# Finished rows handled by pairs, stores on ScalarE's queue, w1's left operands partly in place and left2 held in program order, in a fused graph-attention kernel

## The chip, the cores and the metric

The kernel runs on one core of a Trainium2 chip. The metric is the device time of one execution in microseconds (us); the number quoted for a kernel is the median of its runs. The kernel before takes 1988.92 us, the median of four runs from 1987.42 to 1991.52 on the chip that also ran the changed kernel. (The prediction used 1990.13, the median of three earlier runs.)

## The reference, cut to what matters

Two graph layers on x (4096 x 512), each with a residual and a row norm. The second layer sets the closing stage:

```python
# layer 1; x is the output of layer 0, adj is 4096 x 4096
node_att = softmax(x @ node_w, axis=0)
e = (x @ edge_w) @ (x @ edge_w).T
edge_att = softmax(where(adj > 0, e, NEG_BIG), axis=1)
output = (adj * (node_att * edge_att)) @ (x @ weight) + bias
x = layernorm(x + output)
```

## The kernel before: the parts concerned

The large products are done by Strassen's scheme (seven half-size products in place of eight), which needs sums and differences of operand quarters. Nothing here turns on the algebra; what matters is that TensorE waits for operands which VectorE combines, and that DMAs bring and fetch.

From about 1088 us on the kernel forms the weighted sums `bank <- rop, lop` in sixteen blocks (g, r): four groups g of four blocks. When a group is complete, its rows are *finished*: multiplied with w1 (`po`), added to the residual rows (`xb`), normed and stored. This finishing is cut into small steps (a queue `todo`) that are taken between the sums of the next group, one step for each 8 units of work.

All left operands lie in a pool of four buffers, `lopp`. Three kinds of tile share it before the change: the loads of `lop`, `left2` (combinations of a lop, made by VectorE in the first group only, then stored to memory for the later groups), and `left1` (combinations for w1).

```python
def lefts(self, m, lop):                       # only for g == 0
    s = lopp.tile([P, 4, BG // 2, P], F32, name="left2", tag="lop")
    nc.vector.tensor_add(s1, l21, l22)         # L954
    nc.vector.tensor_sub(s2, s1, l11)          # L955
    nc.vector.tensor_sub(s3, l11, l21)         # L956
    nc.vector.tensor_sub(s4, l12, s2)          # L957
    yield
    nc.scalar.dma_start(to[:, :2]..., lop[:, :, :P])   # ScalarE's queue
    nc.scalar.dma_start(to[:, 2:6], s)
    nc.scalar.dma_start(to[:, 6], l22)
# ...
class Finish:                                  # four row blocks of 128 rows
    def steps(self):
        yield self.load                        # four xb loads, SyncE's queue
        for q in range(2):
            yield from self.pair(q, ps_tr)     # rows (q, q + 2): combine, 7 products
        yield lambda: self.norm(range(BG))     # root, scale and store of all four
# ...
    nc.sync.dma_start(out[...], xb)            # in norm, SyncE's queue
```

The order on each engine is not the order of the program: a scheduler places instructions, except those that are wrapped in `tc.keep_in_program_order`. Before the change that is, in the closing stage, the preparation of operands in the first block (`pinned[0]` is that wrapper for block 0 and does nothing afterwards).

## Time and profile before

Lines L1061 and L1183 of the kernel before are L1062 and L1189 of the changed one (sums and w1 products); L954 to L957 are L955 to L958 (left2); L823 and L835 (mask addition and weighting of the next block's operands) keep their numbers.

My measure throughout is *loss*: the sum of all start-to-start distances of TensorE's records in excess of its own median for the same size (0.429 us for 512 columns, 0.216 for 256, 0.109 for 128). It counts idle time and half-clock time alike. It leaves out places whose excess adds up to 0.1 us or less.

| kernel before, profiled run | loss of TensorE, us |
|---|---|
| 600 to 1083 us (scores, with the hole near 1010) | 12.4 |
| 1083 to 1300 us (first group of blocks) | 7.8 |
| after 1300 us (three holes of 10.6, 11.8 and 12.2 among them) | 44.1 |

The timeline of the kernel before, VectorE and then TensorE (start, length, engine, line, operation, out<-in, shapes, count, and in brackets the idle time before it with what ended it; DVE is VectorE, PE TensorE, ACT ScalarE, POOL GpSimd, SP SyncE, and a q marks the issue of a DMA):

```profile
1167.36 0.43 DVE L954 TENSOR_TENSOR left<-lop 128x256 f32<-128x256 f32 x1 [0.60 <-PE bank L1061]
...
1170.57 0.42 DVE L957 TENSOR_TENSOR left<-lop,left 128x256 f32<-128x256 f32 x1
...
1173.11 2.28 DVE L823 CUSTOM_DVE_ANT_1 lent<-lent,line 128x2048 f32<-128x2048 f32 x1
...
1190.00 8.80 PE L1061 MATMUL bank<-slot,lop 128*128 128x512 f32 x16 [2.07 <-DMA lop<-lop_d]
```

VectorE makes left2 *ahead of* the mask addition L823. ScalarE stores it at 1171.02, that store lands at 1183.93, only then are buffers of the pool free, and SyncE issues three lop loads (1183.99). TensorE waits 2.07 us for the first. So even before the change this chain, left2, store, free buffer, lop load, had no slack at all.

### The profile page before, as it was taken

How to read it: one execution, taken by the hardware profiler on the slowest of the kernel's cores; microseconds unless marked ns; L12 is line 12 of the kernel's file. 1: busy time of each engine (PE TensorE's matmuls, PEld its weight loads, DVE VectorE, ACT ScalarE, POOL GpSimd, SP SyncE). 2: the span in 40 equal slices, each digit the busy share in tenths (PEclk: the TensorE clock that was granted, in tenths of full speed). 3: DMA queues.
4: the chain of work that ended last, by engine and by line, in shares of the span. 5: the costliest groups of instructions: out<-in, count | busy, mean ns of one | idle time of the engine just before them, and what ended most of it. 6: DMA issues, size and time to landing. Idle time of an engine off the chain costs nothing.

```text
span 1990.7 us, 20142 instructions
## 1 busy us (share of the span) xinstructions
PE 1934.7 (97%) x6742; PEld 1210.0 (61%) x6742; DVE 1386.4 (70%) x2050; ACT 1006.0 (51%) x1596; POOL 299.3 (15%) x424
## 2 busy tenths in 40 slices
PE   9999999999999999999989999999899989999898
PEld 6888888888544455545445444466565656666555
DVE  7767667667664575667456974977569866998537
ACT  5433333333104576666567564656656564755621
POOL 0122222223231111111021111110101110111000
PEclk9999999999999999999999999999899999999899
DMA  8888888887465585778598998776668775877621
GB/s 308 301 319 308 305 323 304 306 328 258 171 237 206 201 295 222 262 257 284 204 378 281 338 326 293 261 263 235 240 241 308 259 262 179 318 261 249 247 78 64
DMA packets 153223, 521.82 MB, mean 262 GB/s; under 512 B 15008, under 2 KB 24224, under 8 KB 145440
## 3 DMA queue, kind: packets, MB, share of 16 engines
q1 hardware_dynamic: 66528, 232.68, 34.3%
q0 software_dynamic: 66912, 247.49, 33.4%
q10 hardware_dynamic: 19680, 40.38, 5.7%
q8 instruction: 53, 0.87, 0.2%
q14 instruction: 50, 0.41, 0.1%
HBM read 389.94 MB, written 130.55 MB: 261 GB/s over the span
## 4 chain that ended last, share of the span: by engine, by line
PE 73%; issue 9%; DMA 9%; DVE 6%; ACT 3%; POOL 1%; POOLq 0%; SPq 0%; DVEq 0%; ACTq 0%
PE bank L1061 23%; PE seven L702 13%; PE acc L374 11%; PE acc L373 11%; PE pe L633 4%; PE seven L101 3%; PE po L1183 2%; PE pt L603 2%; DMA slot<-in_adj_t_dram 1%; DMA lop<-lop_d 1%; DMA slot<-s_d 1%; DMA lent<-in_adj_t_dram 1%; DMA out_dram<-xb 1%; PE acc L246 1%; PE pt L333 1%
## 5 line engine op out<-in xcount | busy, mean ns | idle before, releaser
L1061 PE MATMUL bank<-lent,lop 128*128 128x512 f32 (+1 forms) x1292 | 430.6, 485 | 10.8 <-DMA lop<-lop_d 7.7
L373 PE MATMUL acc<-xw,hi 128*128 128x512 f32 x960 | 376.4, 392 | 0.0
L374 PE MATMUL acc<-xw,lo 128*128 128x512 f32 x960 | 374.2, 390 | 0.0
L1061 PE MATMUL bank<-slot,lop 128*128 128x512 f32 (+1 forms) x896 | 349.8, 538 | 3.9 <-DMA lop<-lop_d 2.1
L1061 PEld LDWEIGHTS bank<-lent,lop 128*128 128x128 f32 x1292 | 247.9, 192 | 168.9 <-issue 137.8
L1061 PEld LDWEIGHTS bank<-slot,lop 128*128 128x128 f32 x896 | 171.2, 191 | 157.5 <-issue 142.6
L363 ACT CAST hi<-at 128x1024 fp32r<-128x1024 f32 x120 | 126.4, 1054 | 203.3 <-PE acc L373 148.4
L365 DVE TENSOR_TENSOR lo<-at,hi 128x1024 fp32r<-128x1024 f32 x120 | 146.9, 1224 | 85.2 <-ACT hi L363 85.2
L374 PEld LDWEIGHTS acc<-xw,lo 128*128 128x128 f32 x960 | 180.3, 188 | 37.1 <-DVE lo L365 0.3
L373 PEld LDWEIGHTS acc<-xw,hi 128*128 128x128 f32 x960 | 180.2, 188 | 36.7
L1070 ACT COPY over<-bank 128x512 f32<-128x512 f32 x200 | 114.2, 580 | 143.5 <-PE bank L1061 139.3
L633 PE MATMUL pe<-hT 128*128 128x512 f32 (+3 forms) x384 | 134.3, 493 | 0.0
L574 ACT ACTIVATE line<-line,nmax_c 128x512 f32<-128x512 f32 x160 | 114.9, 725 | 21.8 <-DVE nmax_c L565 21.7
L829 ACT ACTIVATE slot<-slot 128x2048 f32<-128x2048 f32 x40 | 76.5, 1912 | 97.0 <-DMA slot<-in_adj_t_dram 84.9
L565 DVE CUSTOM_DVE_ANT_0 line<-lent,slot 128x512 f32<-128x512 bf16 x144 | 93.1, 688 | 46.6 <-ACT slot L643 22.4
L823 DVE CUSTOM_DVE_ANT_1 slot<-slot,line 128x2048 f32<-128x2048 f32 x36 | 82.2, 2284 | 20.1 <-DMA slot<-s_d 18.7
L1194 DVE SCALAR_TENSOR_TENSOR xb<-po,f,xb 128x256 f32<-128x256 f32 x84 | 40.1, 478 | 75.1 <-PE po L1183 44.9
L826 ACT ACTIVATE slot<-slot 128x2048 f32<-128x2048 f32 x36 | 68.7, 1911 | 45.5 <-DVE slot L823 45.3
L633 PEld LDWEIGHTS pe<-hT 128*128 128x128 f32 x384 | 65.7, 194 | 42.0 <-issue 35.0
L702 PE MATMUL seven<-hT 128*128 128x512 f32 x192 | 89.8, 593 | 0.0
L603 PEld LDWEIGHTS pt<-ident,lent 128*128 128x128 f32 x412 | 51.8, 143 | 61.0 <-issue 46.8
L1037 ACT COPY bank<-over 128x512 f32<-128x512 f32 x144 | 84.4, 593 | 7.1 <-DMA lop<-lop_d 3.1
(258 smaller groups left out, 2879.4 us busy)
## 6 DMA issues: line engine op xcount, KB each, us to landing
at<-in_adj_t_dram SPq DMA_DIRECT2D x60, 1024.0 KB, 6.6
lop<-lop_d SPq DMA_DIRECT2D x112, 512.0 KB, 4.6
slot<-in_adj_t_dram POOLq DMA_DIRECT2D x42, 1024.0 KB, 7.0
slot<-s_d POOLq DMA_DIRECT2D x36, 1024.0 KB, 7.7
s_d<-slot POOLq DMA_DIRECT2D x33, 1024.0 KB, 6.9
lent<-s_d POOLq DMA_DIRECT2D x28, 1024.0 KB, 7.3
lent<-in_adj_dram SPq DMA_DIRECT2D x48, 512.0 KB, 5.1
s_d<-lent POOLq DMA_DIRECT2D x48, 512.0 KB, 4.5
```

What stands on the lines that cost most here:

```text
L363: nc.scalar.copy(hi, aq)
L365: nc.vector.tensor_sub(lo, aq, hi.bitcast(F32))
L373: nc.tensor.matmul(acc, hi[:, c, :], xw[:, kb, :], start=(kb == 0), stop=False)
L374: nc.tensor.matmul(acc, lo[:, c, :], xw[:, kb, :], start=False, stop=(kb == NB - 1))
L565: nc.vector.tensor_tensor_reduce(line, mask, src, -1.0, HUGE, ALU.add, ALU.min, accum_out=nmax_c[:, b, c : c + 1])
L574: nc.scalar.activation(line, line, AF.Exp, bias=nmax_c[:, b, c : c + 1], scale=-1.0, accum_out=sum_c[:, b, c : c + 1])
L603: nc.tensor.transpose(pt[:, j, :], src[:, ts(j, P)], ident)
L633: nc.tensor.matmul(pe[:, lo * P :], hT[:, k, ts(A * BG + i, P)], hT[:, k, (B * BG + lo) * P : (B + 1) * W], start=(k == 0), stop=(k == KD ...
L702: nc.tensor.matmul(ps, left[m][:, k, q, :], right[m][:, k, :], start=(first and k == 0), stop=(k == KD // 2 - 1), skip_group_check=not first,)
L1037: nc.scalar.copy(self.bank[:, : self.w], self.to())
L1061: nc.tensor.matmul(ps, lop[:, k, :], rop[:, k, :], start=start, stop=(k == K - 1), skip_group_check=True)
L1070: nc.scalar.copy(self.to(), self.bank[:, : self.w])
```

## The change

The intent: no block of four stores and four loads in front of the lop loads in SyncE's queue; rows of the other half loaded earlier; fewer tiles in the pool; and left2 held in program order, so that in the first block it no longer runs ahead and blocks VectorE's queue near 1010 us. The diff, cut to its core:

```diff
 def lefts(self, m, lop):
-    nc.vector.tensor_add(s1, l21, l22)
-    ...
+    tc.keep_in_program_order(nc.vector.tensor_add(s1, l21, l22))
+    tc.keep_in_program_order(nc.vector.tensor_sub(s2, s1, l11))
+    tc.keep_in_program_order(nc.vector.tensor_sub(s3, l11, l21))
+    tc.keep_in_program_order(nc.vector.tensor_sub(s4, l12, s2))
 ...
-def steps(self):
-    yield self.load
+def steps(self, then):
     for q in range(2):
         yield from self.pair(q, ps_tr)
-    yield lambda: self.norm(range(BG))
+        some = q, q + 2
+        yield lambda some=some: self.norm(some)
+        yield lambda some=some: (self.scale(some), then and then.load(some))
 ...
 def combine():
-    s.append(lopp.tile([P, 4, KD // 2, P], F32, name="left1", tag="lop"))
-    (four combinations into it)
+    lines.append(take(free_e)); left = lines[0].rearrange(...)   # not from lopp
+    s.extend((l21, s2, s3, l12))
+    nc.vector.tensor_sub(s3, l11, l21)
+    nc.vector.tensor_add(l21, l21, l22)
+    nc.vector.tensor_sub(s2, l21, l11)       # the fourth comes four products later
 ...
-    nc.sync.dma_start(out[...], xb)
+    nc.scalar.dma_start(to, xb)
 ...
-    while owed[0] >= 8: owed[0] -= 8 ...
+    while owed[0] >= 6: owed[0] -= 6 ...
```

There are more steps than before (a norm and a scale for each pair), which is why they come every 6 units of work; with 8 some would be left over at the end and the kernel doesn't build. The joins of inner sums also move one step later (`inner_next`).

## The prediction

> **What bounds the kernel now.** I read the page first, then TensorE's timeline over the closing stage (from 1088 us: the weighted sums in blocks, with the closing rows' products with w1 threaded between them), then the queues' timelines around each hole that it shows. The page says that TensorE is the bound almost everywhere:
>
> ```profile
> PE 1934.7 (97%) x6742; PEld 1210.0 (61%) x6742; DVE 1386.4 (70%) x2050; ACT 1006.0 (51%) x1596; POOL 299.3 (15%) x424
> ```
>
> So the change can only win the holes in TensorE's row, and what follows them. TensorE's timeline shows its pace where nothing waits: a record of 256 columns every 0.216 us (four in 0.86 us), one of 512 every 0.429 us. Comparing every start-to-start distance with this pace, I find 64 us lost after 600 us, 44 us of it after 1290 us, and three holes hold most of that. The first, on TensorE and on SyncE's queue (start, length, engine, line, out<-in, count, idle before):
>
> ```profile
> 1404.73 1.03 PE L1061 MATMUL bank<-slot,lop 128*128 128x256 f32 x4
> 1413.43 3.75 PE L1061 MATMUL bank<-lent,lop 128*128 128x256 f32 x8 [7.67 <-DMA lop<-lop_d]
> 1416.98 1.91 PE L1061 MATMUL bank<-slot,lop 128*128 128x256 f32 x4
> 1418.68 1.18 PE L1183 MATMUL po<-line,left 128*128 128x256 f32 x4
> ...
> 1395.85 2.45 SPq L1238 DMA_DIRECT2D out_dram<-xb  x4
> 1398.35 9.20 SPq L1152 DMA_DIRECT2D xb<-x_d  x4
> 1407.61 0.42 SPq L1049 DMA_DIRECT2D lop<-lop_d  x1
> ```
>
> TensorE waits for left operands (lop). Their load stood in SyncE's queue behind four stores of finished rows (which waited for ScalarE's norm) and four loads of the other half's rows into the same four buffers (which waited for those stores to land). From 1404.73 to the next row at 1419.69 are 14.96 us for 20 records, worth 4.3 us: 10.6 us lost, although the idle is 7.67. The rest is the clock (columns: window, length, busy of PE, PEld, DVE, ACT, POOL, granted clock, DMA share, GB/s):
>
> ```profile
> 1405.00:1414.00 9.00, 1.33 (x6) 0.84 (x5) 4.50 (x5) 5.54 (x9) 0.00 (x0) 0.71 1.04 401
> 1414.00:1419.00 5.00, 5.00 (x13) 4.01 (x12) 2.67 (x3) 1.25 (x3) 0.00 (x0) 0.50 0.17 66
> 1639.00:1648.00 9.00, 7.88 (x13) 3.95 (x14) 8.37 (x7) 1.91 (x1) 0.00 (x0) 0.52 0.45 178
> 1862.00:1870.00 8.00, 6.88 (x12) 3.33 (x11) 8.00 (x13) 1.91 (x1) 0.00 (x0) 0.53 0.36 140
> ```
>
> After each hole TensorE runs some 5 to 8 us at half clock. The other two holes are the same traffic, seen from its other end: here the products wait for VectorE's addition to xb, and that for the late load.
>
> ```profile
> 1626.34 3.19 SPq L1238 DMA_DIRECT2D out_dram<-xb  x4
> 1633.02 2.26 SPq L1152 DMA_DIRECT2D xb<-x_d  x4
> ...
> 1638.30 0.48 DVE L1194 SCALAR_TENSOR_TENSOR xb<-po,f,xb 128x256 f32<-128x256 f32 x1 [8.75 <-DMA xb<-x_d]
> ...
> 1638.84 2.08 PE L1183 MATMUL po<-line,left 128*128 128x256 f32 x4 [6.43 <-DVE xb L1194]
> ...
> 1854.54 2.30 SPq L1152 DMA_DIRECT2D xb<-x_d  x4
> ...
> 1861.35 2.07 PE L1183 MATMUL po<-line,left 128*128 128x256 f32 x4 [7.14 <-DVE xb L1194]
> ```
>
> By the same subtraction the second loses 11.8 us (20.83 us from 1631.39 to 1652.22, with 10 records of 256 and 16 of 512 worth 9.0), the third 12.2 us. A fourth hole lies earlier, where the left combinations of the first block were moved forward by the scheduler and block VectorE's queue:
>
> ```profile
> 1014.74 0.43 DVE L954 TENSOR_TENSOR left<-lop 128x256 f32<-128x256 f32 x1 [9.84 <-DMA lop<-lop_d]
> ...
> 1017.03 1.08 PE L603 MATMUL pt<-ident,lent 128*128 128x128 f32 x4 [6.08 <-DVE lent L747]
> ```
>
> It costs 9.2 us: 6.2 idle and 3.0 slow.
>
> **What the Trainium skill says.** "TensorE: Matmul & The Clock Gate", Part 1: The HAM clock gate, has the clock halve after an idle window of about 3.4 us and come back after about as long a busy one. The trace agrees: 0.50 to 0.53 after idles of 7 us; so a removed hole of 7 us is worth 10 to 12. "DMA: Bandwidth & Descriptors", Anatomy of one DMA, has any semaphore wait sit on the issuing sequencer before dispatch: so one waiting issue holds all behind it, which is what SyncE's queue shows. The same page, Issuing engines are not separate DMA queues, says that issuing from another engine saves only the sequencer's time: the stores gain nothing in transport (2.7 us median here), only in not standing before the lop loads. "ScalarE: Activation LUTs", What ACT_TABLE_LOAD costs: 1283 ns; the trace has 1283 ns for each.
>
> **The change part by part.** *Pairs, and stores on ScalarE's queue.* The same 24 stores and 24 loads of 256 KB. Now rows (0, 2) are normed when their pair is done, stored from ScalarE's queue, and the other half's rows (0, 2) are loaded into their buffers while pair (1, 3) is still multiplied (eight steps). So the load has a whole pair of time, and no store stands in SyncE's queue. The loads still do, each waiting for a store to land, so I looked at the built order of the changed kernel and counted TensorE's work at the pace above. The first pair's last product ends 241 us after the first sum; the load that needs its buffers stands behind a lop load whose buffer TensorE frees only at 252, and the lop behind it is first used at 274. Norm, scale and store cost about 10 us from the page's and timeline's durations (table 1.28, root 0.3, two scalings of 0.8, landing 2.7, queueing), so the loads hardly wait, and 20 us remain for what is behind. For the second pair: 270, 283, 309. The third and fourth: 302, 309, 330 and 334, 344, 365. Later groups look alike. All three holes should go: 10.6 + 11.8 + 12.2 = 34.6 us.
>
> *Left combinations of w1 in place.* As many VectorE operations (four of about 0.42 us per pair), but no buffer of the pool of four that the lop loads use: lops can be a full four ahead. No hole names this, so I count 0; it makes the first item safer.
>
> *left2 held in program order.* VectorE's block at 1004 to 1014 goes. But in the built order ScalarE still has, before its copy of the transposes, two stores of that same lop, which wait for its landing at about 1014.7. TensorE then goes on a few us further until transpose buffers run out. I count 2.5 of the 9.2 us.
>
> *Six more norm groups.* ScalarE gets 6 more roots with two table loads each, 6 x (2 x 1.28 + 0.3) = 17 us, and 24 DMA issues of about 0.4 us (as its other issues show), 10 us. It is busy 385 of the 700 us after 1290: 412 is no bound.
>
> *Steps every 6 units of work instead of 8, inner joins one step later.* Every fourth step comes right behind another. Neighbouring steps use different banks, but VectorE has less time to add before a bank is used again: its queue has 2.28 us operations, and small waits for xb (1.73, 0.72) are there already. The later joins spare VectorE waits for ScalarE's copies (15.1 us off the path). I count 3 us of new small waits.
>
> Sum: 34.6 + 2.5 - 3 = 34 us, from 1990 to 1956. About 1.7%.
>
> **The rivals.** *The load now blocks the queue.* If norm and store come 10 us later than I think, xb loads hold the lops again: each of some 12 pair loads could cost up to 5 us, and the result would be 1970 or worse. For it: the loads stand in the same queue still. Against it: the distances above. *The next wait takes the place.* While TensorE stood, VectorE, ScalarE and the big operand loads caught up; without holes the next block's operands may be late. For it: small waits for operand combinations exist (0.33 at 1549, where no large hole is near). Against it: VectorE has 517 busy of these 700 us, 78% if the stretch shrinks by 35. It would return 5 to 15 us: 1961 to 1971. *TensorE waits for VectorE in the denser steps.* Up to 8 us more: 1964. *All goes.* If the fourth hole and the small ones also vanish, 34.6 + 9.2 + some 5: 1942. For it: small waits after 1290 add to 7 us, some from VectorE's backlog.
>
> **Range and chances.** A 2% gain needs 1950.3, 6 us below my point, and asks for most of the fourth hole or no new waits. The large term is well measured; only the new waits are guessed, so the range leans little: 1946 to 1968. Faster by over 2%: 0.22; within 2%: 0.77; slower: 0.01.
>
> **What would show it.** Right: no wait of TensorE over 3 us after 1290, the three half-clock stretches gone, VectorE's waits for the xb load near 0 (30.1 us now), stores on ScalarE's queue beside it. Partly right: TensorE still idles 2 to 4 us near 1010, with ScalarE's store as the cause. Wrong: TensorE waiting for lop loads behind xb loads; or waits for operands or bank copies spread over the blocks, adding to more than 10 us.

## The result, and the profile after

The changed kernel takes 1966.15 us (median of four runs, 1959.41 to 1972.42). Ratios in this document are the mean time of one kernel's runs over that of the other's of the same rounds, so not quite the ratio of the quoted medians: here 0.9884, 95% interval 0.9847 to 0.992. The class, within 2%, and the range hold; the point, 1956, was 10 us too low. The four runs spread over 13 us; the kernel before spreads over 4 us in its four, but over 12 us in the eleven runs timed beside e1 to e4, so the spread by itself says little.

The line of engines on the page of the changed kernel:

```profile
PE 1926.4 (98%) x6742; PEld 1206.2 (61%) x6742; DVE 1389.8 (71%) x2062; ACT 1021.8 (52%) x1614; POOL 300.1 (15%) x424
```

TensorE is busy 8.3 us less for the same 6742 products: that is half-clock time gone. The next view is SyncE's queue where the first of the large holes was (the same point of the work lies some 20 to 30 us earlier or later from kernel to kernel):

```profile
1371.06 1.13 SPq L1154 DMA_DIRECT2D xb<-x_d  x2
1372.29 0.67 SPq L1050 DMA_DIRECT2D lop<-lop_d  x1
...
1400.81 1.18 SPq L1154 DMA_DIRECT2D xb<-x_d  x2
1402.08 1.62 SPq L1050 DMA_DIRECT2D lop<-lop_d  x2
```

Two loads at a time, 1.1 us each pair, in place of the block of four stores and four loads that held the queue from 1395.85 to 1407.55. They still wait for stores to land (68.0 us in 18 waits in the list of SyncE's waits), but that time is taken from slack: no product waits for xb or lop there. Table of windows (length, busy of PE, PEld, DVE, ACT, POOL, granted clock, DMA share, GB/s), the changed kernel:

```profile
1187.00:1199.00 12.00, 1.45 (x3) 0.50 (x2) 9.60 (x6) 7.41 (x10) 0.75 (x1) 0.71 1.03 403
1199.00:1203.00 4.00, 4.00 (x7) 1.59 (x6) 3.36 (x6) 0.83 (x1) 0.00 (x0) 0.58 0.53 193
1395.00:1409.00 14.00, 14.00 (x57) 10.63 (x56) 13.87 (x18) 9.38 (x15) 0.75 (x1) 1.00 0.83 287
1840.00:1860.00 20.00, 20.00 (x77) 14.26 (x76) 15.33 (x24) 16.20 (x24) 2.25 (x3) 1.00 0.71 242
```

The last two rows, at places where large holes were, show TensorE full at full clock. The first two show a hole that was not there before: 1.45 us of work in 12 us. In numbers, the loss after 1300 us fell from 44.1 to 11.1 us, that of 1083 to 1300 grew from 7.8 to 19.2, and that of 600 to 1083 fell from 12.4 to 10.2. The sum falls by 23.8 us; the medians by 22.8.

The new hole, in the timelines of VectorE, ScalarE's queue, SyncE's queue and TensorE of the changed kernel:

```profile
1174.55 2.29 DVE L823 CUSTOM_DVE_ANT_1 lent<-lent,line 128x2048 f32<-128x2048 f32 x1 [8.57 <-DMA lent<-s_d]
...
1178.96 0.42 DVE L955 TENSOR_TENSOR left<-lop 128x256 f32<-128x256 f32 x1
...
1182.17 0.42 DVE L958 TENSOR_TENSOR left<-lop,left 128x256 f32<-128x256 f32 x1
...
1182.62 0.34 ACTq L962 DMA_DIRECT2D lop_d<-left  x1
...
1190.70 0.80 SPq L1046 DMA_DIRECT2D lop<-lop_d  x2
...
1198.25 2.04 PE L1062 MATMUL bank<-slot,lop 128*128 128x512 f32 x2 [10.55 <-DMA lop<-lop_d]
```

It is the chain shown of the kernel before, but left2 now comes *behind* L823, which stood 8.57 us for the load of s, and behind an L835. So left2 begins at 1178.96 in place of 1167.36, its store is issued 11.6 us later (1182.62 against 1171.02), lands at 1190.64, and the lop loads behind it land from 1198.12 on. Not all of the 11.6 us is the holding: the lop that left2 is made from landed at 1170.76 here and at 1167.28 before. The cleaner comparison is e3 below, where it landed at 1171.15. In the built order this is the work of `keep_in_program_order`, which the scheduler had not had to respect for left2 before.

The hole near 1010 is smaller but there; ScalarE and its queue, changed kernel:

```profile
1014.36 0.39 ACTq L961 DMA_DIRECT2D lop_d<-lop  x1
1014.78 1.04 ACTq L963 DMA_DIRECT2D lop_d<-lop  x1
1015.87 0.59 ACT L604 COPY slot<-pt 128x512 f32<-128x512 f32 x1 [9.90 <-issue]
```

ScalarE's copy of the transposes stands 9.9 us behind its own two issues, which wait for a lop to land. TensorE stands 4.7 us for that copy; the loss is 7.3 us where it was 9.2.

### The profile page after: what moved, and what is told of

Its sections match the earlier page's. It is cut to its first block, busy times and chain, and to the rows that moved or that the text cites.

```text
span 1966.4 us, 20188 instructions
## 1 busy us (share of the span) xinstructions
PE 1926.4 (98%) x6742; PEld 1206.2 (61%) x6742; DVE 1389.8 (71%) x2062; ACT 1021.8 (52%) x1614; POOL 300.1 (15%) x424
## 4 chain that ended last, share of the span: by engine, by line
PE 69%; DVE 11%; DMA 9%; issue 8%; ACT 2%; POOL 1%; ACTq 0%; POOLq 0%; DVEq 0%; SPq 0%
PE bank L1062 19%; PE seven L702 13%; PE acc L373 11%; PE acc L374 11%; PE pe L633 5%; PE po L1189 3%; PE pt L603 2%; DMA slot<-s_d 2%; PE seven L101 2%; DMA lop<-lop_d 1%; DVE lent L835 1%; DMA lent<-s_d 1%; DVE over L1125 1%; DMA slot<-in_adj_t_dram 1%; DMA lop_d<-left 1%
## 5 line engine op out<-in xcount | busy, mean ns | idle before, releaser
L1062 PE MATMUL bank<-lent,lop 128*128 128x512 f32 (+1 forms) x1292 | 425.2, 480 | 0.0
L1062 PE MATMUL bank<-slot,lop 128*128 128x512 f32 (+1 forms) x896 | 351.0, 540 | 13.4 <-DMA lop<-lop_d 10.5
L823 DVE CUSTOM_DVE_ANT_1 slot<-slot,line 128x2048 f32<-128x2048 f32 x36 | 82.3, 2287 | 31.8 <-DMA slot<-s_d 31.4
L823 DVE CUSTOM_DVE_ANT_1 lent<-lent,line 128x2048 f32<-128x2048 f32 x28 | 64.0, 2285 | 33.7 <-DMA lent<-s_d 23.9
L604 ACT COPY slot<-pt 128x512 f32<-128x512 f32 (+3 forms) x126 | 69.7, 556 | 31.7 <-PE pt L603 21.7
```

Of the source, the lines that this page charges most:

```text
L823: pinned[0](nc.vector._custom_dve(TENSOR_ADD_SAT, out=q, in0=q, in1=m, s0=0.0, s1=-HUGE))
L1062: nc.tensor.matmul(ps, lop[:, k, :], rop[:, k, :], start=start, stop=(k == K - 1), skip_group_check=True)
```

## The experiments

All twelve runs gave correct results. Each was timed on the same chip as runs of the kernel before; losses are those of the one profiled run.

| run | median, us (lowest to highest) | ratio to before, 95% interval | loss 600-1083 | 1083-1300 | after 1300 |
|---|---|---|---|---|---|
| before | 1988.92 (1987.42 to 1991.52) | 1 | 12.4 | 7.8 | 44.1 |
| changed | 1966.15 (1959.41 to 1972.42) | 0.9884 (0.9847 to 0.992) | 10.2 | 19.2 | 11.1 |
| e1 | 1951.38 (1949.42 to 1956.38) | 0.981 (0.9787 to 0.9833) | 11.8 | 7.0 | 6.8 |
| e2 | 1995.56 (1988.34 to 2000.14) | 1.0026 (1.0003 to 1.0048) | 10.1 | 15.0 | 41.9 |
| e3 | 1951.63 (1949.78 to 1952.54) | 0.9808 (0.9786 to 0.9829) | 10.0 | 9.1 | 3.3 |
| e4 | 1962.26 (1956.37 to 1965.7) | 0.9854 (0.9831 to 0.9878) | 9.0 | 11.5 | 8.5 |
| e5 | 1953.56 (1949.11 to 1956.12) | 0.9814 (0.9792 to 0.9835) | 5.9 | 11.6 | 5.5 |
| e6 | 1980.73 (1978.5 to 1988.31) | 0.9959 (0.9932 to 0.9986) | 13.9 | 10.1 | 36.1 |
| e7 | 1959.77 (1957.01 to 1962.58) | 0.9847 (0.9824 to 0.987) | 8.4 | 11.4 | 12.3 |
| e8 | 1955.43 (1951.95 to 1957.32) | 0.9823 (0.9804 to 0.9843) | 10.6 | 11.3 | 7.8 |
| e9 | 1952.18 (1947.18 to 1954.74) | 0.9812 (0.979 to 0.9833) | 7.5 | 8.7 | 4.9 |
| e10 | 1955.6 (1952.48 to 1955.84) | 0.9828 (0.981 to 0.9847) | 7.0 | 15.5 | 5.0 |
| e11 | 1955.69 (1951.48 to 1961.07) | 0.9839 (0.9816 to 0.9862) | 10.6 | 11.7 | 2.9 |
| e12 | 1962.26 (1957.45 to 1964.73) | 0.9862 (0.984 to 0.9884) | 9.7 | 11.9 | 11.4 |

(The expectations of the first four runs give the loss from 1088 to 1300 and leave out clusters under 0.15 us: 6.9 for before and 17.8 for the changed kernel.)

**e1: left2 free again.** The changed kernel without the holding.

```diff
-            tc.keep_in_program_order(nc.vector.tensor_add(s1, l21, l22))
+            nc.vector.tensor_add(s1, l21, l22)
             (and the three others)
```

> The changed kernel with one part undone: the four left2 operations are no longer held in program order. My theory is that this holding makes the new hole of 10.7 us at 1187 (VectorE stood 8.6 us for the load of s ahead of left2, so the store of left2 to memory and the lop loads behind it came late) and part of the holes around 1100, and that it saves only 1.9 us of the hole at 1010. Theory: TensorE's loss between 1088 and 1300 falls from 17.8 to 7-9 us, the hole near 1010 grows from 7.3 to about 9.2, the time falls from 1966 to 1955-1960, a ratio of about 0.984 to the kernel before. Rival (the loss comes from the denser steps or from the way the large loads fall): loss of 1088-1300 stays over 14 us and the time at 1964-1970.

The hole at 1187 is gone, the loss from 1083 to 1300 is 7.0, the hole near 1010 loses 8.3 us. The interval of its ratio lies clear of that of the changed kernel. So the holding is what makes the hole at 1187 and costs time; but my number was off: 1951.4 in place of 1955 to 1960 (and 5.6 in place of 7 to 9 in the measure of the expectation), since the loss after 1300, where no left2 is made, also fell, from 11.1 to 6.8.

**e2: the holding alone, in the kernel before.**

```diff
-            nc.vector.tensor_add(s1, l21, l22)
+            tc.keep_in_program_order(nc.vector.tensor_add(s1, l21, l22))
             (and the three others)
```

> The kernel before with this one part alone: left2 held in program order. Theory: the loss between 1088 and 1300 grows from 6.9 to about 15-18 us, the hole near 1010 shrinks by about 2 us, the three holes after 1400 stay at 10-12 us each, and the time is 1995-2000, ratio 1.003 to 1.005. Rival (the holding is harmless by itself, and the loss needs the rest of the change): time 1986-1990, ratio 0.998 to 1.000, loss between 1088 and 1300 of about 7 us.

Close to the theory: the loss at 1187 is 8.4 us (4.0 before), the loss of 1083 to 1300 is 15.0 (13.4 in the measure of the expectation, a little under its 15 to 18), that near 1010 falls from 9.2 to 7.2, the late holes stay. The time is 5 us longer, an interval just clear of 1. So the hole at 1187 needs nothing else of the change; what the holding goes with after 1300 in the changed kernel (see e12) doesn't appear here.

**e3: left2 held in the first block only.**

```diff
-            tc.keep_in_program_order(nc.vector.tensor_add(s1, l21, l22))
+            pinned[0](nc.vector.tensor_add(s1, l21, l22))
             (and the three others; pinned[0] holds in block 0 and does nothing after it)
```

> The changed kernel with left2 held in program order only while the first block is recorded; in the later blocks the scheduler is free. In the built order this moves the left2 of the second block ahead of VectorE's mask addition that waits for the load of s. Theory: the hole at 1187 goes or shrinks to about 2 us as in the kernel before, the hole near 1010 stays at 7.3, the holes around 1100 (4.8 us together) stay; time 1955-1959, ratio 0.983 to 0.985, the best so far. Rival: the hole at 1187 stays over 8 us since it comes from the loads of s, and the time is 1964-1970.

The three timelines of e3, VectorE, SyncE's queue, TensorE, at the place of the new hole:

```profile
1171.34 0.42 DVE L955 TENSOR_TENSOR left<-lop 128x256 f32<-128x256 f32 x1 [7.45 <-DMA lop<-lop_d]
...
1177.10 2.29 DVE L823 CUSTOM_DVE_ANT_1 lent<-lent,line 128x2048 f32<-128x2048 f32 x1
...
1179.20 3.05 SPq L1046 DMA_DIRECT2D lop<-lop_d  x3
...
1181.74 13.90 PE L1062 MATMUL bank<-slot,lop 128*128 128x512 f32 x32
```

left2 stands ahead of L823 again, the lop loads are issued at 1179.20 in place of 1190.70, and TensorE runs 32 products without a gap. 1951.63 us, faster than both kernels, with a spread of under 3 us; against the kernel before the interval, 1.7 to 2.1% less, lies across the mark of 2%. The hole at 1187 went, as the theory had it, and the time fell below its 1955 to 1959. It isn't faster than e1: holding left2 in the first block is worth 1 us at 1010 and nothing that the times show.

**e4: the stores back on SyncE's queue.**

```diff
-                    nc.scalar.dma_start(to, xb)
+                    nc.sync.dma_start(to, xb)
```

> The changed kernel with the stores of the finished rows back on SyncE's queue; pairs, steps and all else stay. What I said in the prediction: the stores gain by not standing before the lop loads. If the pairs do most of the work (norm, scale and store of a pair come about 30 us before the lop is needed), there is little loss: TensorE's loss after 1300 stays under 16 us (11.1 now), time within 4 us of 1966. If the other queue does it, holes of over 3 us with TensorE waiting for lop return after 1400, two per group of finished rows: loss after 1300 over 25 us, time 1980 or more. I hold the first for likelier, 65 to 35.

No hole returns (loss after 1300 8.5 us), and the time is no worse. So it is not the queue that removed the holes. That leaves the rest of the change, and of it I take the pairs with their early loads. This is by elimination: e7 and e8 undo two other parts (the second only in part, 7 units in place of 8), no run undoes the pairs alone, and the later joins were not tested. The hole at 1187 lost 2.7 us in this profile, with left2 held in all blocks: its size varies, which led to e12.

**e5: ScalarE's three issues held as well, in the first block.**

```diff
-            nc.scalar.dma_start(to[:, 2:6], s)
+            pinned[0](nc.scalar.dma_start(to[:, 2:6], s))
             (and the two others; on the kernel of e3)
```

> The kernel of e3, in which also ScalarE's three issues that store the first left operands and left2 are held in program order while the first block is recorded. In the built order this takes two of these issues from in front of ScalarE's copy of the transposes; TensorE's order is the same. Theory, that of the prediction: what remains of the hole near 1010 is ScalarE's issue, which waits until 1014.8 for the load of lop to land, with the copies behind it. Then the loss of 7.3 us near 1010 to 1022 falls under 2 us, and the time falls from 1951.6 to 1944-1947. Rival (TensorE meets the next wait, for VectorE's row statistics or for transpose buffers): the loss stays over 4 us, the time over 1948.5.

The loss is the theory's, the time is over the rival's 1948.5. Near 1010 TensorE now runs through, so ScalarE's blocked queue *was* the rest of that hole: shown. But the time did not follow. SyncE's queue and TensorE of e5:

```profile
1109.50 0.81 SPq L1046 DMA_DIRECT2D lop<-lop_d  x2
...
1113.57 8.82 PE L1062 MATMUL bank<-lent,lop 128*128 128x512 f32 x14 [3.82 <-DMA lop<-lop_d]
```

The stores of the first lop, issued at 1014 to 1016 in the changed kernel, now come at 1103 to 1104, and its buffer is free only then. TensorE loses 6.6 us for it at 1109 to 1118, where e3 loses nothing. By the table the loss before 1083 is 4.1 us less than in e3, that to 1300 2.5 us more and that after it 2.2 us more: what was gained at 1010 was handed back, most visibly 100 us later through the pool of four.

**e6: only the stores on ScalarE's queue, in the kernel before.**

```diff
-                nc.sync.dma_start(out[...], xb)
+                (nc.sync if self.last else nc.scalar).dma_start(out[...], xb)
```

> The kernel before, with the stores of the finished rows on ScalarE's queue and nothing else (but for the last rows, as in the change). The loads of the next rows still stand in SyncE's queue before the lop load and still wait for those stores to land. Theory: the three holes stay, 8 to 12 us each, loss after 1300 over 35 us, time 1983-1992. Rival (the stores' own time in SyncE's queue was the harm): holes shrink to under 5 us each, loss after 1300 under 25 us, time under 1975.

In between, nearer to the theory: the holes lose 8.6, 7.4 and 4.7 us, others of 5.5 and 2.8 us appear, and the loss after 1300 is 36.1 us. The four loads still hold SyncE's queue in front of the lop loads, for 9.55 us at 1403.86 (9.20 before). So the queue alone is worth some 8 us to the kernel before (ratio 0.9959, by its interval 3 to 14 us), which is more than I had said, but only a quarter of the 33 us of loss that the whole change removes after 1300.

**e7: left1 in the pool again, on the kernel of e3.**

```diff
-                s.extend((l21, s2, s3, l12))
+                left = lopp.tile([P, 4, KD // 2, P], F32, name="left1", tag="lop")
+                s.extend(left[:, n] for n in range(4))
                 (four combinations into it, as before the change)
```

> The kernel of e3 with the left combinations of w1 again as four operations into a buffer of the pool of lop loads, as before the change. In the prediction I counted 0 for their removal. Theory: since a combination takes a pool buffer for eight steps, some lop loads are only issued when few buffers are left; with the row loads early there is slack: loss after 1300 is 3-7 us (3.3 in e3), time 1951-1956. Rival (the freed buffer is what makes the change work): holes with TensorE waiting for lop return, loss after 1300 over 15 us, time over 1962.

Neither is right. The time is 1959.8, 8 us more than e3, and the loss after 1300 12.3 in place of 3.3; but TensorE hardly waits more for lop (3.5 us in three waits, 2.0 in two in e3). It waits for VectorE's addition. Two lists of waits (engine, line, waited for: us in total, times, longest), first of e7, then of e3:

```profile
PE po L1184 <- DVE xb L1195: 10.2, 6, 3.2
```

```profile
PE po L1189 <- DVE xb L1200: 1.8, 3, 0.8
```

So the combinations in place are worth about 8 us on the kernel of e3, by way of VectorE (the two intervals still touch, at 0.9824 to 0.9829). The run changes two things at once, the pool buffer and the place of the fourth combination, which comes back in front of the first product; they were not told apart. How it acts is not settled either: at the largest of these waits VectorE's addition stood behind a mask addition that waited 5.50 us for a load of s, and the runs don't tell why that load was later.

**e8: steps every 7 units of work, on the kernel of e3.**

```diff
-            while owed[0] >= 6:
-                owed[0] -= 6
+            dense = 7 if n < 12 else 6
+            while owed[0] >= dense:
+                owed[0] -= dense
```

> The kernel of e3 with a step every 7 units of work, in place of 6, up to the twelfth block (8, as before the change, leaves steps over at the end). I predicted 3 us of new small waits from denser steps. In e3 TensorE loses only 3.3 us in all after 1300, so at most that can be had: theory now, time 1949-1953, no difference to e3. If the prediction's term were real, loss after 1300 would fall by 1-2 us.

It is 4 us slower if anything, just above my 1949 to 1953, with intervals that overlap, and the loss after 1300 rose to 7.8 us. The denser steps cost nothing that this can find, as far as 7 against 6 tells.

**e9: the combinations of w1's right operand later, on the kernel of e3.**

```diff
-        if n == 1:
-            todo.append(lambda: nc.vector.tensor_sub(t3, r22, r12))
+        if n == 2:
+            todo.append(lambda: tc.keep_in_program_order(nc.vector.tensor_sub(t3, r22, r12)))
             (and the three others)
```

> The kernel of e3 with VectorE's four combinations of w1 moved from the second block to the third and held in program order there. In e3 they run at 1094.5 to 1097.4, ahead of the combination that TensorE waits for (3.28 us idle at 1101, 5.1 us lost until 1107). Theory: that combination comes 3 us earlier (four of 0.69 us), the loss near 1100 falls from 5.1 to under 2.5 us, time 1947.5-1950 against 1951.6. Rival (something else is met there, such as the next load): loss near 1100 over 4 us, time over 1950.5.

A mixed result: the loss near 1100 falls as expected, from 5.1 to 1.4 us, but 1.3 us stand at 1109, 1.7 at 1200 and 4.4 at 1230 (2.1 in e3) instead, and that near 1010 is 3.6 (7.3); the sum of losses is 21.1 in place of 22.4, and the median of 1952.2 doesn't move.

**e10: e5 and e9 together.**

> The kernel of e5 (ScalarE's three issues held in the first block, too) with the w1 combinations later as in e9. In e5 the hole near 1010 was gone, but 3.0 us at 1092 and 6.6 us at 1109 to 1118 stood there instead; the second is the wait for a lop load whose buffer was freed by a later store of the first left operands (issued at 1103 to 1104). Theory: with VectorE 3 us earlier both shrink, loss of 1083 to 1300 from 11.6 to 5-8 us, time 1944-1949, the best of all. Rival (the store issue time, not VectorE, sets the second): loss over 9 us, time 1949-1953.

The rival holds for the loss, which is 15.5 us from 1083 to 1300. With VectorE earlier the hole at 1110 to 1120 is 7.7 us (6.6 in e5): the lop load is issued at 1111.07, when ScalarE's late store of left2 has landed (1111.02). The time, 1955.6 us, is above both ranges.

**e11: stores on SyncE's queue, on the kernel of e3.**

> The kernel of e3 with the stores of finished rows on SyncE's queue: the same question as e4, now without the noise of the hole at 1187. e4 (1962.3) was no slower than the change (1966.2). Theory: with pairs and the early load, the queue makes no difference: 1949-1955, loss after 1300 of 3-8 us. Rival (ScalarE's queue is worth something, as in e6, where it took 8 us off the kernel before): time 1957 or more, with lop waits of TensorE after 1300.

1955.7, just over my 1949 to 1955 and under the rival's 1957; the loss after 1300 is 2.9 us, no hole returns, and the interval overlaps that of e3. Here SyncE's queue is 4 us slower by the medians, in e4 it was 4 us faster: with pairs, no worth of the queue is shown.

**e12: the changed kernel once more.**

> The changed kernel itself, once more, for its spread and a second trace. Its first four runs lay from 1959 to 1972, while e1 and e3 spread over 3 to 7 us. Theory: the loss at 1187 depends on how long the store of left2 and the two lop loads behind it take to land, so it differs from run to run: here between 2 and 13 us, with the time following it, 1956-1972. If instead the hole is a fixed 10 us, the time is 1964-1968 with the hole of 10 us again. The loss of 4.5 us at 1329 I expect to be gone or different (luck of the transfers).

1962.3. The hole at 1187 lost 4.3 us here and 12.8 in the first trace. The order is the same: left2 begins at 1173.29, since the load of s came sooner (VectorE stood 6.09 us for it, not 8.57). So the size of this hole goes with how late the loads in flight land. In these two traces it accounts for the difference in time as well (8.5 us at the hole, 7.9 us in time); there are no more to tell whether the whole spread comes with it. Windows of e12, before and behind the gap:

```profile
1188.00:1190.50 2.50, 0.10 (x1) 0.01 (x1) 0.50 (x1) 2.50 (x3) 0.75 (x1) 1.00 1.03 406
1190.50:1194.00 3.50, 3.48 (x4) 1.50 (x5) 3.35 (x2) 0.61 (x2) 0.00 (x0) 0.51 1.03 400
```

Here an idle of 2.42 us was followed by 3.5 us at half clock. The loss at about 1321 to 1334, which I had put down to luck, came again (4.5 us, then 4.7). It is 2.4 us in e4, the third trace of the changed kernel's steps with left2 held in all blocks, and absent in e1 and e3, so it too goes with the holding. The trace of the changed kernel, VectorE and then TensorE, shows its last part:

```profile
1320.52 2.29 DVE L823 CUSTOM_DVE_ANT_1 slot<-slot,line 128x2048 f32<-128x2048 f32 x1 [4.13 <-DMA slot<-s_d]
...
1332.02 2.05 PE L1189 MATMUL po<-line,line 128*128 128x256 f32 x4 [2.59 <-DVE xb L1200]
```

The addition to xb that TensorE waits for (L1200) stands in VectorE's queue behind mask additions, and these wait for loads of s. GpSimd issued the two loads concerned within 0.8 us of each other (1311.24 and 1311.98; in e12 1303.14 and 1303.88), in e3 6 us apart (1296.33 and 1302.37). Why the holding brings them together stays open.

## Why the prediction was right or wrong, point by point

**The three holes: right.** Predicted 34.6 us; the loss after 1300 fell by 33.0. The windows at full clock and SyncE's short visits to xb show the mechanism, and VectorE's waits for the load of xb (30.1 us before) are gone from the list of waits. What carries it are, by elimination, the pairs with the early load: e4 and e11 keep the gain without the other queue, e6, with the queue alone, wins 8 us, and e7 and e8 bring no large hole back. No run has the pairs alone.

**"No hole names this, so I count 0" (left1 out of the pool): mis-sized.** In e7 it measured about 8 us, though not as a wait for lop, and together with the place of one combination. Whether the prediction's total missed them can't be told: they act on small waits, which it had counted as 3 us the other way.

**"I count 2.5 of the 9.2 us" (the hole near 1010): right.** 1.9 us were saved in the first trace (2.0 in e2; in later traces with the same holding the hole still lost 3.6 to 7.3 us, so the saving varies), and e5 shows ScalarE's store as the cause of the rest, as written.

**Left2 in program order: the step that failed.** I looked only at what the holding repairs, in the first block, and gave it no cost. The operations are recorded in all four blocks of the first group, and holding them there puts left2 behind mask additions that wait for loads. That cost 12.8 us at 1187 in the first trace and 4.3 in the second. In all, taking it away after the first block is worth 10.6 to 14.5 us of the median (e12 and the first runs against e3, on different chips, with intervals of the ratios that lie apart); with the stores on SyncE's queue (e4 against e11) it is 6.6 us, and those intervals overlap. The chain at 1187 is only a part of it: against e3 the changed kernel loses 10.1 us more from 1083 to 1300 and 7.8 us more after 1300, e12 2.8 and 8.1 us. The share after 1300 is traced only as far as e12 shows. In the prediction's terms, the loss after 1300 fell by 33.0 us for the 31.6 foreseen (34.6 less 3), that before 1083 by 2.2 for 2.5, and that between rose by 11.4 for 0: so the predicted 1956 becomes the measured 1966. The changed order had been at hand, and showed left2 behind L823; I read it only around the holes that I knew.

**"3 us of new small waits" (denser steps): wrong, near 0.** e8 finds none, and in e3 all loss after 1300 is 3.3 us, where before the small holes alone, outside the three large ones, held 9.5 (44.1 less 34.6). In the changed kernel itself 11.1 us remained there, but 7.8 of them are gone in e3, with the same steps.

**ScalarE: right.** It is busy 15.8 us more (1021.8 less 1006.0; predicted 17 without the issues), and no hole after 1290 waits for it.

**The rivals.** "The next wait takes the place" came true in its number (1961 to 1971), and that is luck: the 11 us stand in the first group, which has no finished rows at all, and not behind the holes removed, and e1 shows that they come from the holding. The kernel of e3, 1951.6 with the hole near 1010 still there, lies between the point (1956) and "All goes" (1942).

## What to carry to other kernels

When an instruction is held in program order, read the built order for each place where it is recorded, and ask what now stands in front of it and whether that waits for a transfer; here a wait ahead of an operation that frees a shared buffer showed up as a late load some 20 us on. Split a batch of norm, store and load into pairs when the next batch uses the same buffers: here that, by elimination, and not the choice of queue, removed 33 us of loss. And a hole closed early can be paid again through a small pool: look at the time, not only at the hole.

## What the Trainium skill lacked or had wrong

- "TensorE: Matmul & The Clock Gate", Part 1: The HAM clock gate, ties the lower clock to at least one idle window of about 3.4 us. Here shorter idles were enough: 2.42 us (e12, granted clock 0.51 for the next 3.5 us) and 2.85 us (changed kernel at 1103, 0.55 for the next 3.8 us). But length alone did not decide it: 2.07 us were enough in the kernel before at 1188 (0.57 from 1190 to 1192), while after 2.34 us there at 1103, 2.51 us in e4 at 1186 and 3.35 us in e9 at 1010 the granted clock stayed at 1.00. After every idle of over 3.4 us in these traces, from 500 us on, it fell. So in counting what a hole of 2 to 3.4 us costs, a slow tail is possible and not certain.
- "DMA: Bandwidth & Descriptors", Anatomy of one DMA, fits the time of a transfer from GpSimd's queue as about 2.0 us plus bytes over 436 GB/s, which makes an estimate of 4.4 us for 1024 KB. The medians of its frequent transfers of this size here are 6.6 to 7.9 us (changed kernel), and VectorE's wait for one load differed by 2.5 us between two runs of the same kernel. The page's own table for this queue (Bandwidth, Measured) has 6.15 us for 1 MB, which is above its fit and nearer to these medians; a number for a transfer among others I did not find there.
- The same page, Issuing engines are not separate DMA queues, puts the gain of another issuing engine at the time to issue. Two things are missing there. An issue that waits holds the compute work of its engine: ScalarE's copy stood 9.90 us behind two of them. And taking stores out of a queue in which other loads wait was worth some 8 us in e6, and nothing that is shown once the batch was split (4 us one way in e11 against e3, 4 us the other in e4 against the changed kernel).
